# ScalarE issues part of the single-row transfers: eleven tiles fetched by rows, not eight

## The chip, the cores and the metric

The kernel runs on one core of a Trainium2 chip. The metric is the device time of one execution in microseconds (us): the median of the runs before the change is 726.54 us (three runs, 725.65 to 727.59). Engines are named as in the profile: PE is TensorE (PEld its weight loads), DVE VectorE, ACT ScalarE, POOL GpSimd, SP SyncE. A "q" behind a name is that engine's own queue: the instructions which it handles itself, among them the issue of transfers (DMAs).

## The reference

One layer of a graph network on 12,500 nodes with 128 features and 400,000 edges that are sorted by destination, followed by a residual and a layer norm.

```python
rbf = jnp.exp(-(distances[:, None] - centers) ** 2 / (2.0 * width * width))
cut = 0.5 * (jnp.cos(jnp.pi * distances / CUTOFF) + 1.0) * (distances <= CUTOFF)
W = (silu(rbf @ fw1 + fb1) @ fw2 + fb2) * cut[:, None]
messages = (h[src] @ pw + pb) * W
agg = segment_sum(messages, dst, num_segments=num_atoms)
h2 = h + (silu(agg @ mw1 + mb1) @ mw2 + mb2)
out = layernorm(x + h2)
```

Edges with a distance over 10 give nothing. The costly access is `h[src]`: one row of 512 bytes for each edge that counts.

## The kernel before

**Stages.** First `h @ pw + pb` is computed for all nodes and stored in HBM as the table `proj` (the first twelve tiles of edges still read the input's rows instead, which are multiplied in place). Meanwhile DVE drops the edges beyond the cutoff, chunk by chunk (seven chunks), and POOL stores the remaining ones packed; SP loads each packed chunk back (`pair`, L789), and from it come the source indices `srci` (L878), the local destinations `dl`, the cutoff factors and the distances, which are stored as `near_d` (L865).

**The loop.** What remains is 139 tiles of 512 edges, each of four rows of 128. The main loop (`for q in range(NL - 1)`) handles one tile a step:

- `fetch` (L1016): POOL fetches 128 rows of `proj` by an indirect DMA, four of them a tile, into a place of `quad_sb` (or of `x`). There are 21 places for the first 63 tiles and nine afterwards. `fetches` writes as many of them as have a free place by the planner's clock.
- `radials` (L1030): SP loads the distances of a pair of tiles (an "oct"), spread over partitions, into `d`, of which there are three buffers.
- `basis` (L1057, L1058): ACT squares and exponentiates them (`rbf`), for two octs at every fourth step. `first` (L1066): PE multiplies `rbf` with `fw1` into `ph`, of which there is one buffer. `silu` (L1072): ACT. `second` (L1080, L1083): PE, for the tile two steps ahead.
- `message` (L1094): DVE multiplies the filter in PSUM with the fetched rows. `place` (L1106): DVE writes a one-hot matrix of destinations. `sum_up` (L1126): PE sums messages by destination with it. `add` (L1160): DVE adds finished windows into `aggT`.
- Node stages run between (L1169 to L1224); SP loads and stores their tiles (L171).

**Tiles by rows.** For the eight tiles of `SINGLY` POOL makes three fetches, not four. The first 128 rows are brought row by row by SP: `one_by_one` (called once a step) writes single-row DMAs of 512 bytes into `dl_0` (L1006), one for each `A_ROW` = 0.58 us of the planner's clock. Their addresses are registers, loaded 32 at a time from `at_row` (L1002). DVE multiplies these rows in an instruction of its own (L1092).

**Order.** Each engine works its instructions in the order in which they stand in its queue. The order is set where the kernel is built, from the source's order by a scheduler. Hardware transfers of SP and ACT take eight completion semaphores ("places") in turn; a transfer that takes a place waits until the one before it in that place has landed. In the kernel before ACT issues six transfers, all near the start, and SP all others of that kind.

Of the kernel before, what the change touches and what calls it, by code (L numbers as in the profile page):

```python
# [10 lines left out]
F32 = mybir.dt.float32  # L11
BF16 = mybir.dt.bfloat16
I32 = mybir.dt.int32
U8 = mybir.dt.uint8
# [6 lines left out]
P = 128  # L21
# [8 lines left out]
QE = QT * P  # L30
# [51 lines left out]
def kernel(  # L82
# [37 lines left out]
    nc = tc.nc  # L120
    N, H = x.shape
# [44 lines left out]
    def node_dma(t0, sb, dr, store, n=None, eng=nc.sync):  # L166

        for a, m, k in alike(rows(t0, n)):
            d = dr[(t0 + a) * P:(t0 + a) * P + m * k].rearrange("(p t) f -> p t f", p=k)
            s = sb[:k, a:a + m]  # L170
            eng.dma_start(d, s) if store else eng.dma_start(s, d)  # L171

    raw = {}

    def load_rows(c):

        raw[c] = []
        of = (("r_src", src, I32), ("r_d", edge_weight, I32), ("r_dst", dst, I32))
        for name, ap, dt in of if c == 0 else of[1:] + of[:1]:
            t = work.tile([P, R_MAX], dt, name=name, bufs=2)[:, :ROWS[c]]  # L180
            v = ap[P * sum(ROWS[:c]):P * sum(ROWS[:c + 1])].rearrange("(r l) -> r l", r=P)
            nc.sync.dma_start(t, v if ap is not edge_weight else v.bitcast(I32))
            raw[c].append(t)
        if c == 0:
            raw[c].append(raw[c].pop(0))
# [12 lines left out]
    zero_i = keep.tile([P, 376], I32, name="zero_i")  # L198
    packed = dram.tile([LISTS, MW], I32, name="packed")

    def clear_packed(k, eng):
        a, b = CLEAR[k:k + 2]
        for i in range(LISTS if k == 0 else 3):
            v = packed[i, a:b].rearrange("(p w) -> p w", p=P)
            for w0 in range(0, (b - a) // P, 376):
                n = min(376, (b - a) // P - w0)
                eng.dma_start(v[:, w0:w0 + n], zero_i[:, :n])

    aggT = keep.tile([P, N], F32, name="aggT")

# [11 lines left out]

    def load(name, shape, ap, eng=nc.sync):
        t = keep.tile(shape, F32, name=name)
        eng.dma_start(t, ap)
        return t

    def load_bias(name, ap, eng=nc.sync):
# [5 lines left out]
    for t0 in range(0, 16, 4):  # L234
# [5 lines left out]
    loads = [(w1_sb[2 * a + h:2 * b - 1 + h:2, h, :], ap) for h in (0, 1)  # L240
             for a, b, ap in ((0, NUM_RBF, fw1), (NUM_RBF, KR, row(fb1)))]
# [152 lines left out]
    clock = [4.3]  # L394
# [106 lines left out]
    def pack_first():  # L501
# [124 lines left out]
        free.append(at)  # L626
        by_row = near_d[:p_d].rearrange("r (j p) -> (r j) p", j=2)
        for a, b in parts(D):
            nc.sync.dma_start(by_row[a:b], turned_d[a:b])
# [149 lines left out]
    def unpack(c):  # L779
# [6 lines left out]
        pair = work.tile([64, 3, 512], I32, name="pair", bufs=1)  # L786

        def listed(t, a, b, l0, l1):
            (nc.scalar if c < 1 else nc.sync).dma_start(t[a:b, :l1 - l0],  # L789
                              packed[l0:l1, (p0 + a) * 512:(p0 + b) * 512]  # L790
                              .rearrange("s (p w) -> p s w", w=512))

# [66 lines left out]
        def lengths():  # L859

            if c < 2:
                alike_in(1)
            one_of(length, 1)
            for a, b in parts(np_):
                nc.sync.dma_start(near_d[p0 + a:p0 + b], length[a:b].bitcast(F32))  # L865
            stored.add(c)

        def to_places(f, to):
# [119 lines left out]
        return own_sb[name, k]  # L988

    own_sb = {}  # L990
    singles, alone, rows_at, row_at = [], {}, [], [0.0]

    def one_by_one():

        row_at[0] = max(row_at[0], clock[0] - 8.0)
        while singles and row_at[0] < clock[0]:
            row_at[0] += A_ROW
            q, e, i = singles.pop(0)
            if e == 0:
                alone[q] = dl_0[:, SINGLY.index(q) % 4, :]  # L1000
            if e % AT_ONCE == 0:
                _, rows_at[:] = nc.values_load_multi_w_load_instructions(  # L1002
                    i[:, e:e + AT_ONCE], engines=[mybir.EngineType.SP], min_val=0,
                    max_val=(N - 1) * 4 * H, skip_runtime_bounds_check_because=
                    "sources are at most N - 1 where they are copied")
            nc.sync.dma_start(alone[q][e:e + 1, :].bitcast(U8),  # L1006
                              proj.rearrange("n f -> (n f)").bitcast(U8)[ds(rows_at[e % AT_ONCE], 4 * H)]
                              .rearrange("(o f) -> o f", o=1))

    def fetch(q, idx=None, table=None, js=range(QT)):  # L1010
        got = quad_sb[place_of(q) if q >= 0 else 0]
# [13 lines left out]
    def radial(o, lengths):  # L1025

        n = math.prod(lengths.shape) // QE
        d = work.tile([P, QE], F32, name="d", bufs=3)
        v = lengths.rearrange("(o h) e -> o h e", o=1)
        nc.sync.dma_start(d, v.to_broadcast([64, 2, QE]))  # L1030
        d_of[o] = d, n

    next_o = [0]
# [14 lines left out]
    def basis(o):  # L1048
        if o not in d_of:
            for q in quads(o):  # L1050
                while chunk_of(q) not in stored:
                    go_on(todo[0])
            radials(o + 1)
        d, n = d_of.pop(o)
        u = 2 * KR
        rbf = work.tile([P, QE], F32, name="rbf")
        nc.scalar.activation(rbf[:u], d[:u], AF.Square, bias=rbf_bias[:u], scale=rbf_scale[:u])  # L1057
        nc.scalar.activation(rbf[:u], rbf[:u], AF.Exp, scale=-1.0 / (2.0 * width * width))  # L1058
        rbf_of[o] = rbf, n
# [27 lines left out]
    def message(q, js=(0, QT)):  # L1087
        msg = own(q, "msg", 0)
        a, b = js
        if q in SINGLY and a == 0:  # L1090
            assert q in alone and all(s[0] != q for s in singles)
            nc.vector.tensor_mul(msg[:, 0, :], pu_of[q][:, :H], alone.pop(q))  # L1092
            a = 1
        nc.vector.tensor_mul(msg[:, a:b, :], pu_of[q].rearrange("p (j f) -> p j f", j=QT)[:, a:b, :],  # L1094
                             got_of[q][:, a:b, :])
        if b == QT:
            free.append(pu_of.pop(q))
            got_of.pop(q)
        return msg
# [285 lines left out]
    for k, t0 in enumerate(tiles):  # L1385
        if k + AHEAD_X < len(tiles):
            load_x(tiles[k + AHEAD_X], 4)
        if loads and k >= 4 and k % 2 == 0:
            nc.sync.dma_start(*loads.pop(0))
# [61 lines left out]
    for q in range(NL - 1):  # L1451
# [8 lines left out]
        if q >= CLEAR_Q:  # L1460
            clear()
        if loads_later and q >= 8:
            nc.sync.dma_start(*loads_later.pop(0))
# [92 lines left out]
    def everything():  # L1556
        nc.vector.memset(aggT, 0.0)
        def again(e0, seen):

            def column(ap, dt, name):  # L1560
                t = work.tile([P, QT], dt, name=name, bufs=1)
                nc.sync.dma_start(t, ap[ds(e0, QE)].rearrange("(j p) -> p j", p=P))
                return t

            idx = column(src, I32, "idx")
# [81 lines left out]
```

## Time and profile before

| | |
|---|---|
| runs | 726.54 us median, 725.65 to 727.59 |
| profiled execution | 726.45 us, its span 724.6 us |
| granted PE clock, mean | 0.912 |
| busy: PE, PEld | 586.3 us (81%), 463.4 us (64%) |
| busy: DVE, ACT, POOL | 560.9 us (77%), 403.9 us (56%), 532.7 us (74%) |
| fetches of POOL (L1016) | 405 + 95 + 48 = 548, 949 to 985 ns each |
| single rows of SP (L1006) | 1024, and 32 index loads |

"Busy" is the sum of an engine's instructions without register work, semaphores and the issue of transfers; those stand under the engine's "q". A group of the page's costliest instructions reads: line, engine, operation, what it writes from what, how many; then busy time and mean ns of one; then the engine's idle time just before them, with what ended most of it ("issue": nothing that the profile shows). A row of the timeline reads: start in us from the span's start, duration, engine, line, operation, tiles, how many in a row, and in brackets the idle time before it. A row of the windows reads: stretch, its length, then busy time and number of instructions for each engine named, and last granted clock, share of DMA and GB/s. A row of the waits reads: who waited for whom: us in total, times, longest. A row of one line's instructions reads: minimum, median and maximum in ns, then first and last start.

### The profile page before, as it was taken

What the parts mean: (1) busy time and instruction counts of PE and PEld (TensorE: products, weight loads), DVE (VectorE), ACT (ScalarE), POOL (GpSimd) and SP (SyncE); (2) the same over time, 40 slices, a digit from 0 to 9 for tenths busy, and PEclk for the clock granted to TensorE, in tenths of its full rate; (3) what the DMA queues carried; (4) which work ended last, traced back from release to release, by engine and by line L of the source; (5) the groups of instructions that cost most, each with busy time, mean ns of one, the idle gap of its engine ahead of it and who ended that gap; (6) DMA issues with size and microseconds to landing.
All of it is one profiled execution on the core that took longest, in us unless ns stands there. A gap on an engine that the chain in (4) does not pass through costs nothing.

```text
span 724.6 us, 13518 instructions
## 1 busy us (share of the span) xinstructions
PE 586.3 (81%) x3531; PEld 463.4 (64%) x3531; DVE 560.9 (77%) x1734; ACT 403.9 (56%) x573; POOL 532.7 (74%) x569
## 2 busy tenths in 40 slices
PE   6778868698889787598758896999896788797874
PEld 6666557676667566477536684877674566575753
DVE  8899799689999898699969794967556455564774
ACT  7547625364556566275444467557645744374683
POOL 6777777777777777777777777777777777777770
PEclk9998788899999899699988999899899988999996
DMA  8995442443334332433334344534443433345251
GB/s 278 324 314 182 146 125 75 112 115 96 100 90 127 98 94 74 147 93 89 98 102 113 100 125 121 158 98 138 115 112 98 141 98 109 102 122 149 57 154 56
DMA packets 53104, 91.38 MB, mean 126 GB/s; under 512 B 13824, under 2 KB 20576, under 8 KB 53018
## 3 DMA queue, kind: packets, MB, share of 16 engines
q1 hardware_dynamic: 34610, 53.34, 22.2%
q0 software_dynamic: 17840, 36.77, 20.5%
q8 instruction: 30, 0.49, 0.3%
q14 instruction: 56, 0.46, 0.2%
q10 hardware_dynamic: 568, 0.33, 0.2%
HBM read 74.59 MB, written 15.79 MB: 125 GB/s over the span
## 4 chain that ended last, share of the span: by engine, by line
DVE 29%; PE 19%; POOL 16%; DMA 14%; issue 14%; ACT 5%; DVEq 2%; SPq 1%; ACTq 0%; POOLq 0%
POOL quad L1016 14%; DMA quad<-proj,srci 8%; DVE hot L1106 6%; PE ph L1066 4%; PE bank L1083 4%; DVE msg L1094 3%; PE sums L1126 3%; PE bank L328 3%; POOL x L1016 2%; DVE aggT L1160 2%; DVE bank L492 2%; DVE nodes L496 2%; DVE r_d L486 2%; DMA x<-proj,srci 1%; DVEq L1135 1%
## 5 line engine op out<-in xcount | busy, mean ns | idle before, releaser
L1016 POOL DMA_INDIRECT quad<-proj,srci x405 | 384.5, 949 | 123.5 <-issue 98.8
L1083 PEld LDWEIGHTS bank<-fw_sb,s 128*128 128x128 f32 x1112 | 159.2, 206 | 61.5 <-issue 51.2
L1072 ACT ACTIVATE s<-ph 128x1024 f32<-128x1024 f32 x70 | 71.3, 1018 | 160.7 <-PE ph L1066 160.6
L1083 PE MATMUL bank<-fw_sb,s 128*128 128x128 f32 x1112 | 159.3, 290 | 0.0
L1066 PE MATMUL ph<-rbf,w_sb 102*128 102x512 f32 x278 | 138.8, 623 | 10.6 <-ACT s L1072 6.5
L1126 PEld LDWEIGHTS sums<-hot,msg 128*128 128x128 f32 x816 | 110.0, 201 | 50.1 <-issue 25.3
L1126 PE MATMUL sums<-hot,msg 128*128 128x80 f32 (+4 forms) x816 | 112.9, 284 | 10.5 <-DVE msg L1094 10.2
L1106 DVE TENSOR_SCALAR hot<-iota_n,dl,cut 128x80 f32<-128x80 f32 (+4 forms) x408 | 108.8, 339 | 14.7 <-PE sums L1126 12.9
L1016 POOL DMA_INDIRECT x<-proj,srci x95 | 90.8, 956 | 29.0 <-issue 24.1
L1080 PE MATMUL bank<-fb_b,ones_b 96*128 96x512 bf16 x139 | 56.1, 404 | 42.7 <-DVE msg L1094 15.6
L1094 DVE TENSOR_TENSOR msg<-bank,quad 128x512 f32<-128x512 f32 (+1 forms) x78 | 52.8, 677 | 43.0 <-DMA quad<-proj,srci 32.3
L1066 PEld LDWEIGHTS ph<-rbf,w_sb 102*128 102x128 f32 x278 | 49.2, 197 | 46.9 <-issue 35.2
L1160 DVE TENSOR_TENSOR aggT<-aggT,sums 128x80 f32 (+4 forms) x209 | 53.9, 258 | 28.0 <-PE sums L1126 11.9
L1057 ACT ACTIVATE rbf<-d,rbf_bias,rbf_scale 102x512 f32<-102x512 f32 x70 | 56.2, 803 | 33.3 <-DMA d<-near_d 33.3
L1016 POOL DMA_INDIRECT quad<-in_x_dram,srci x48 | 47.3, 985 | 15.4 <-issue 12.5
L328 PEld LDWEIGHTS bank<-pw_sb,xT 128*128 128x128 f32 (+1 forms) x292 | 41.6, 206 | 10.8 <-issue 5.5
L1094 DVE TENSOR_TENSOR quad<-bank,quad 128x512 f32<-128x512 f32 (+2 forms) x40 | 25.2, 633 | 28.2 <-DMA quad<-proj,srci 23.7
L1072 ACT ACT_TABLE_LOAD x36 | 46.2, 1283 | 0.6
L1126 PE MATMUL sums<-quad,quad 128*128 128x128 f32 (+3 forms) x296 | 44.9, 302 | 1.6 <-DVE quad L1094 1.5
L1058 ACT ACT_TABLE_LOAD x35 | 44.9, 1283 | 0.6
L1058 ACT ACTIVATE rbf<-rbf 102x512 f32<-102x512 f32 x70 | 44.1, 630 | 1.5
L1126 PEld LDWEIGHTS sums<-quad,quad 128*128 128x128 f32 x296 | 42.5, 220 | 2.4 <-DVE quad L1094 2.2
(268 smaller groups left out, 816.6 us busy)
## 6 DMA issues: line engine op xcount, KB each, us to landing
d<-near_d SPq DMA_DIRECT2D x70, 256.0 KB
dl<-proj SPq DMA_DIRECT2D x1024, 0.5 KB
x<-in_x_dram SPq DMA_DIRECT2D x46, 256.0 KB
quad<-proj,srci POOLq DMA_INDIRECT x405
proj<-hp SPq DMA_DIRECT2D x24, 256.0 KB
out_dram<-x SPq DMA_DIRECT2D x22, 256.0 KB
x<-proj,srci POOLq DMA_INDIRECT x95
r_d<-in_edge_weight_dram SPq DMA_DIRECT2D x5, 256.0 KB
```

The source lines that it names most:

```text
L328: nc.tensor.matmul(to[:m, k, :], lT[:, k * P:k * P + m], w, start=False, stop=(k == a + c - 1))
L1016: nc.gpsimd.indirect_dma_start(out=got[:, j, :], out_offset=None, in_=proj if table is None else table, in_offset=bass.IndirectOffsetOnAxi ...
L1057: nc.scalar.activation(rbf[:u], d[:u], AF.Square, bias=rbf_bias[:u], scale=rbf_scale[:u])
L1058: nc.scalar.activation(rbf[:u], rbf[:u], AF.Exp, scale=-1.0 / (2.0 * width * width))
L1066: nc.tensor.matmul(ph[:, h, :], w1_sb[:2 * KR, h, :], rbf[:2 * KR], start=True, stop=True)
L1072: nc.scalar.activation(s[:, :n], ph[:, :n], AF.Silu)
L1080: nc.tensor.matmul(pu, ones_b[:, :P], bias_b["fb2"].rearrange("k j f -> k (j f)"), start=True, stop=False)
L1083: nc.tensor.matmul(pu[:, j * H:(j + 1) * H], s[:, j * P:(j + 1) * P], fw2_sb, start=False, stop=(j == QT - 1))
L1094: nc.vector.tensor_mul(msg[:, a:b, :], pu_of[q].rearrange("p (j f) -> p j f", j=QT)[:, a:b, :], got_of[q][:, a:b, :])
L1106: nc.vector.tensor_scalar(hot[:, j, :wide(q)], iota_n[:, :wide(q)], dl[:, at[0], at[1]], cut[:, at[0], at[1]], op0=OP.is_equal, op1=OP.mult)
L1126: nc.tensor.matmul(pa[:, k * W:k * W + wide(q)], msg[:, j, :], hot[:, j, :wide(q)], start=(j % n == 0), stop=(j % n == n - 1))
L1160: nc.vector.tensor_add(to, to, pa[:, k * W:k * W + wide(q)])
```

## The change

`SINGLY` holds eleven tiles, spread over the loop. All hardware transfers go through `issue`, which counts them as they are written. When SP would write one whose number is 3 or 7 modulo 8 (`ACT_LANES`) and rows are pending, ACT writes a row first, which takes that number; so, counted in the order of writing, ACT's rows always have the numbers 3 and 7. Each engine loads its own indices: SP 32 at a time, ACT eight (`ACT_AT_ONCE`). `one_by_one` is called at three points of a step, with 2.8, 1.4 and 0 us subtracted from the planner's clock. The message of a tile by rows is unchanged.

```diff
-SINGLY = (22, 45, 62, 67, 86, 102, 118, 133)
+SINGLY = (20, 30, 43, 57, 68, 81, 95, 108, 118, 127, 135)
 A_ROW = .58
+ACT_LANES = (3, 7)
+ACT_AT_ONCE = 8
...
+    issued, singles, due = [0], [], {}
+
+    def issue(eng, to, frm):
+
+        while eng is nc.sync and (singles or due.get(nc.scalar)) and issued[0] % 8 in ACT_LANES:
+            one_row(nc.scalar, ACT_AT_ONCE)
+        issued[0] += 1
+        eng.dma_start(to, frm)
...
-                singles.extend((q, e, at_row[p:p + 1]) for e in range(P))
+                singles.append([q, 0, at_row[p:p + 1]])
...
-    def one_by_one():
+    def one_by_one(us):
 
         row_at[0] = max(row_at[0], clock[0] - 8.0)
-        while singles and row_at[0] < clock[0]:
+        while (singles or due.get(nc.sync)) and row_at[0] < clock[0] - us:
             row_at[0] += A_ROW
...
+            one_row(nc.sync, AT_ONCE)
+
+    def one_row(eng, n):
+
+        if not due.get(eng):
+            q, e, i = singles[0]
+            n = min(n, P - e)
             if e == 0:
-                alone[q] = dl_0[:, SINGLY.index(q) % 4, :]
+                alone[q], left[q] = dl_0[:, SINGLY.index(q) % 4, :], P
+            singles[0][1] += n
+            if e + n == P:
+                singles.pop(0)
+            _, at = nc.values_load_multi_w_load_instructions(
+                i[:, e:e + n], engines=[eng.engine], min_val=0, max_val=(N - 1) * 4 * H,
...
+            due[eng] = [(q, e + k, at[k]) for k in range(n)]
+        q, e, at = due[eng].pop(0)
+        left[q] -= 1
+        issue(eng, alone[q][e:e + 1, :].bitcast(U8),
+              proj.rearrange("n f -> (n f)").bitcast(U8)[ds(at, 4 * H)]
+              .rearrange("(o f) -> o f", o=1))
...
         radials(q // 2 + 5)
-        one_by_one()
+        one_by_one(2.8)
...
+        one_by_one(1.4)
         if q > NL - 5:
             keep_busy(2)
         sum_up(q, msg)
...
             add(k)
+        one_by_one(0.0)
         tail(q)
```

All other `nc.sync.dma_start(...)` of the kernel become `issue(nc.sync, ...)`.

More of the change, by code (lines that the diff above doesn't have):

```diff
@@ L170, in node_dma @@
             s = sb[:k, a:a + m]
-            eng.dma_start(d, s) if store else eng.dma_start(s, d)
+            issue(eng, d, s) if store else issue(eng, s, d)
     raw = {}
@@ L181, in load_rows @@
             v = ap[P * sum(ROWS[:c]):P * sum(ROWS[:c + 1])].rearrange("(r l) -> r l", r=P)
-            nc.sync.dma_start(t, v if ap is not edge_weight else v.bitcast(I32))
+            issue(nc.sync, t, v if ap is not edge_weight else v.bitcast(I32))
             raw[c].append(t)
@@ L224, in load @@
         t = keep.tile(shape, F32, name=name)
-        eng.dma_start(t, ap)
+        issue(eng, t, ap)
         return t
@@ L628, in pack_first @@
         for a, b in parts(D):
-            nc.sync.dma_start(by_row[a:b], turned_d[a:b])
+            issue(nc.sync, by_row[a:b], turned_d[a:b])
         yield 0.3
@@ L788, in listed @@
         def listed(t, a, b, l0, l1):
-            (nc.scalar if c < 1 else nc.sync).dma_start(t[a:b, :l1 - l0],
+            issue(nc.scalar if c < 1 else nc.sync, t[a:b, :l1 - l0],
                               packed[l0:l1, (p0 + a) * 512:(p0 + b) * 512]
@@ L864, in lengths @@
             for a, b in parts(np_):
-                nc.sync.dma_start(near_d[p0 + a:p0 + b], length[a:b].bitcast(F32))
+                issue(nc.sync, near_d[p0 + a:p0 + b], length[a:b].bitcast(F32))
             stored.add(c)
@@ L990 @@
     own_sb = {}
-    singles, alone, rows_at, row_at = [], {}, [], [0.0]
-    def one_by_one():
+    alone, left, row_at = {}, {}, [0.0]
+    def one_by_one(us):
         row_at[0] = max(row_at[0], clock[0] - 8.0)
-        while singles and row_at[0] < clock[0]:
+        while (singles or due.get(nc.sync)) and row_at[0] < clock[0] - us:
             row_at[0] += A_ROW
-            q, e, i = singles.pop(0)
-            if e == 0:
-                alone[q] = dl_0[:, SINGLY.index(q) % 4, :]
[L1001 to L1008, printed above, removed]
+            one_row(nc.sync, AT_ONCE)
[3 more added lines that the diff above has]
+            n = min(n, P - e)
+            if e == 0:
+                alone[q], left[q] = dl_0[:, SINGLY.index(q) % 4, :], P
[4 more added lines that the diff above has]
+                i[:, e:e + n], engines=[eng.engine], min_val=0, max_val=(N - 1) * 4 * H,
+                skip_runtime_bounds_check_because=
+                "sources are at most N - 1 where they are copied")
+            due[eng] = [(q, e + k, at[k]) for k in range(n)]
[4 more added lines that the diff above has]
+              .rearrange("(o f) -> o f", o=1))
     def fetch(q, idx=None, table=None, js=range(QT)):
@@ L1090, in message @@
         if q in SINGLY and a == 0:
-            assert q in alone and all(s[0] != q for s in singles)
+            assert q in alone and left[q] == 0
             nc.vector.tensor_mul(msg[:, 0, :], pu_of[q][:, :H], alone.pop(q))
@@ L1388 @@
         if loads and k >= 4 and k % 2 == 0:
-            nc.sync.dma_start(*loads.pop(0))
+            issue(nc.sync, *loads.pop(0))
         if k == 2:
```

8 lines of the change are left out of this document (4 added, 4 removed).

## The prediction

> **What bounds the kernel now.** First the page's head, its slices, and its costliest group.
>
> ```profile
> span 724.6 us, 13518 instructions
> ...
> POOL 6777777777777777777777777777777777777770
> ...
> L1016 POOL DMA_INDIRECT quad<-proj,srci x405 | 384.5, 949 | 123.5 <-issue 98.8
> ```
>
> POOL's digit is 7 from beginning to end, and its idle time before a fetch is "issue": it waits for nothing. The timeline of POOL and its fetches counted in two stretches give the pitch.
>
> ```profile
> 131.78 0.99 POOL L1016 DMA_INDIRECT quad<-proj,srci  x1 [0.30 <-issue]
> ...
> 704.33 0.94 POOL L1016 DMA_INDIRECT quad<-proj,srci  x1 [0.30 <-issue]
> ```
>
> ```profile
> 130.00:500.00 370.00, 276.37 (x291) 0.92 0.38 108
> 500.00:706.00 206.00, 155.27 (x164) 0.93 0.41 116
> ```
>
> 455 fetches stand in the two stretches; between the two shown lie 457 steps (453 fetches, four stores of packed rows): 572.55 / 457 = 1.253 us each. The last fetch ends at 705.27, and 19.3 us of span follow it. So POOL sets the end if the loop keeps up. Whether it does: the messages (L1094, one a tile) in the same stretches, all engines there, and the waits after 500 us.
>
> ```profile
> 130.00:500.00 370.00, 59.76 (x89) 0.92 0.38 108
> 500.00:706.00 206.00, 29.69 (x45) 0.93 0.41 116
> ```
>
> ```profile
> 500.00:706.00 206.00, 171.36 (x983) 129.88 (x983) 122.21 (x418) 118.92 (x173) 155.27 (x164) 0.93 0.41 116
> ```
>
> ```profile
> DVE msg L1094 <- DMA quad<-proj,srci: 32.3, 15, 4.7
> DVE quad L1094 <- DMA quad<-proj,srci: 23.2, 13, 3.2
> ```
>
> Before 500 us the loop goes at its own pace, 370 / 89 = 4.16 us a tile, while POOL needs 4 x 1.253 = 5.01: the loop eats POOL's lead and catches it near 500. After that DVE waits 55.5 us for landing fetches (28 times). That is the loop's **spare**: at most these 55.5; at least 206 - 45 x 4.16 = 19; PE's idle time there is 206 - 171.4 = 34.6. I take 35, PE being the busiest engine there. A loop that falls behind by less than its spare costs nothing at the end.
>
> SyncE issues all other transfers. Its instructions, two rows of its timeline, its waits over the span, and two landings from the chain that ended last:
>
> ```profile
> L1002 SPq TENSOR_LOAD <-at_row x32: 2107/2157/2347, 76.4 to 645.9; - x32
> ```
>
> ```profile
> L1006 SPq DMA_DIRECT2D dl<-proj x1024: 227/228/413, 79.1 to 664.1; - x171
> ```
>
> ```profile
> L1030 SPq DMA_DIRECT2D d<-near_d x70: 518/521/1362, 51.0 to 664.4; - x70
> ```
>
> ```profile
> 482.57 0.53 SPq L1030 DMA_DIRECT2D d<-near_d  x1
> 483.21 4.38 SPq L1006 DMA_DIRECT2D dl<-proj  x13
> ```
>
> ```profile
> SPq L171 <- ACT x L1224: 68.7, 16, 23.2
> SPq L789 <- DMA packed<-line,at_i: 30.3, 5, 9.2
> SPq L1006 <- DMA d<-near_d: 15.6, 31, 1.2
> ```
>
> ```profile
> 228.38 2.97 DMA d<-near_d
> ...
> 377.41 2.23 DMA dl<-proj
> ```
>
> A row takes 4.38 / 13 = 0.337 us of SP, an index load 2.16. From 79.1 to 664.4 SP has 585 us; 1024 rows are 345, 32 index loads 69, and some 142 other transfers (64 d loads at .56; 78 at .42, by the two pair loads in .77 shown below; each with a gap of .04) 68: 482 in all, so SP is busy 82% of the time. The 15.6 us in 31 waits of rows for a d load are the rule of places at work: a transfer may start only when the one before it in its place, eight transfers earlier, has landed. A row in its place finds 8 x .337 = 2.7 us past, more than 2.23; behind a d load it does not.
>
> **The change, part by part.** *Fetches.* Three more tiles by rows take three fetches off POOL: 3 x 1.253 = **-3.76 us**, certain if POOL stays the bound.
>
> *Rows.* 11 x 128 = 1408. In the built kernel SP still issues 1024, ScalarE 384, with 48 index loads of eight values. SP's own issue thus stays at 482. On ACT the nearest price of an index load is one of a single value:
>
> ```profile
> L1514 ACTq TENSOR_LOAD <-bad_i x1: 792/792/792, 699.6 to 699.6; - x1
> ```
>
> ```profile
> 699.62 0.38 ACT L1171 ACTIVATE zs<-bank 128x256 f32<-128x256 f32 x1 [1.09 <-PE bank L1169]
> ```
>
> ```profile
> ACT s L1072 <- PE ph L1066: 160.6, 58, 7.4
> ```
>
> .79, then; SP's 32 values cost 2.16; by the nearer I take 1.0 for eight. 48 x 1.0 + 384 x .26 (DMA and MOVE as on SP) = 148 us of ACT's queue. The two rows show how ACT's queue stands: zs waited 1.09 us for PE, and the load behind it came only as zs started, then ran beside it. So a row is **held by a waiting ACTIVATE** and is free beside a running one. ACT idles 160.6 us before the silus alone, so the issue by itself costs the loop little: 0 (all beside running work) to 20, taken as 5 in the pairs' sum below.
>
> The Trainium skill has it otherwise (Perfetto Trace Analysis, DVE / Act Engine Instruction): a vector or scalar instruction goes into a wait queue, and the sequencer takes the next one while the semaphores are still awaited. By that rule ACT's rows would not be held; the trace disagrees here, 699.62 against 699.6. What the rule would give in time is A's 722.8, below.
>
> *Places.* In the order in which the kernel is written ACT's rows take the fourth and eighth place of each turn. In the built program the eight places are dealt out in the scheduler's order instead, and there ACT's 384 rows lie in all eight, 39 to 61 in each. 301 of SP's transfers come in a place that ACT used last; 236 of these wait for an ACT row that the source wrote later than them, by 42 instructions in the median (a loop step has some 65). 299 ACT rows wait for one of SP's. So the two queues now run in **lockstep**, where before SP ran ahead.
>
> What it costs SP: I added up both queues in their built order with the prices above and nothing else (no compute on ACT), each transfer starting when its queue is free and its place has landed (2.23 after a row, 2.97 after others). Before: 481 us without places, 522 with them. That leaves 585 - 522 = 63 for waits on others' work; the table shows 30.3 of it at L789 and part of L171's 68.7. After: 485 without, **588** with places, 66 more than before. The bounds: if all 63 us of the old waits fall inside new ones, 588 - 585 = 3 us later; if none do, 66. With landings of 2.5 and 3.5 (the waits behind d loads allow this) it would be 85. Since ACT's compute, which holds rows, is not in the count, I go near the upper of the first two: **50**.
>
> A second way to it, by pairs of octs. The ACT timeline of a pair, one later second rbf, and all waits of that kind:
>
> ```profile
> 430.07 0.80 ACT L1057 ACTIVATE rbf<-d,rbf_bias,rbf_scale 102x512 f32<-102x512 f32 x1
> ...
> 432.72 0.80 ACT L1057 ACTIVATE rbf<-d,rbf_bias,rbf_scale 102x512 f32<-102x512 f32 x1
> ...
> 488.72 0.80 ACT L1057 ACTIVATE rbf<-d,rbf_bias,rbf_scale 102x512 f32<-102x512 f32 x1
> ```
>
> ```profile
> ACT rbf L1057 <- DMA d<-near_d: 33.3, 11, 7.1
> ```
>
> In 27 of 30 pairs of the new order the second d load stands, through its place or that of an SP transfer ahead of it, behind an ACT row just before the first rbf, 432.72 - 430.07 = 2.65 us ahead of the rbf that reads it. The row (.26), its landing (2.23), SP's work between (1.5 in the mean of the order) and the landing of d (2.97) make 6.96; less 2.65, and less up to 1.02 when the row goes out beside the silu ahead: 3.3 to 4.3 us late. Before, that load came early (482.57 for the rbf at 488.72: 6.15, less 2.97 = 3.2 to spare) and only 11 of 70 waited. PE notices when ACT's slack is gone, 160.6 / 58 = 2.8 a silu: .5 to 1.5 a pair, 16 to 46 over 31 pairs. With the late pair load of chunk 2 (below, 0 to 5 each for five chunks, 8 taken) and ACT's issue, 5, that is 29 to 59. Both ways lie about 45: 50 less the 3.2 us that SP was ahead is **47 us of lateness**, of which 35 go into the spare: **+12** at the end.
>
> *Pair loads.* They are hurried where a chunk begins:
>
> ```profile
> 117.96 0.77 SPq L789 DMA_DIRECT2D pair<-packed  x2
> ```
>
> ```profile
> 119.57 1.02 ACT L1072 ACTIVATE s<-ph 128x1024 f32<-128x1024 f32 x1 [0.94 <-PE ph L1066]
> ```
>
> ```profile
> 124.28 0.46 DVE L807 TENSOR_TENSOR two<-pair 44x256 int32<-44x256 int32 x1
> ...
> 129.25 0.24 DVE L878 CAST srci<-bank 128x88 int32<-128x88 f32 x1
> ```
>
> In the new order the load of 117.96 stands behind an ACT row that follows the silu of 119.57: 119.6 + three rows (.8) + 2.23 = 122.6, some 4.7 us later, and lands at 122.6 + .8 + 2.97 = 126.4, 2.1 after DVE began on it at 124.28. The indices, ready at 129.49, come 2.1 to 4.7 later, and POOL, which first reads them at 131.78, has 2.3 to spare: it may starve 0 to 2.4 us. I count 0 for POOL, the rest above.
>
> *Other edits.* Three calls of the pacing function instead of one spread SP's rows; their count is the same: nothing, and at most the 482 us shift within a step. The rows are written six steps or more (6 x 4.16 = 25 us) ahead of their message, so they themselves come in time if SP is late by less.
>
> Sum: the profiled run has span 724.6 and takes 726.45, the median of the runs is 726.54: 726.54 - 3.76 + 12 = **734.8**.
>
> **Rivals.**
> A, *the lateness stays inside the spare*: POOL bounds, 726.54 - 3.76 = **722.8**. For: 55.5 us of waits for fetches, ACT's 160.6 idle, the low end of either count (3, 29). It is also the time if ACT's rows are not held, as SP then finds them landed. Against: SP at 82% with its 63 us tied to others' work, and the order of places. Turning point: lateness 35.
> B, *even*: POOL starves 2.4 at chunk 2, and the lateness passes the spare by some 1: 722.8 + 3.4 = **726.2**. It needs two numbers to fall in a narrow band.
> C, *the holds feed one another*: an ACT row waits for an SP transfer that stands behind an SP row held by ACT. In the count ACT's own rows have 46 such changes of queue on the longest chain. With landings 2.5 and 3.5, excess 85, less 3, less the spare's low end 19: +63, **786**; slower still than forecast.
> D, *the rows do sit in two places*: then SP meets only its own transfers in six places, 6 x .337 = 2.02 us a turn against a landing of 2.23, .21 over 1024 / 6 = 171 turns: 36 us, which SP's 585 - 482 = 103 free us can take: **722.8** again. The built order speaks against it.
>
> **How the numbers follow.** The forecast, loop later than its spare, .57 (727.5 to 766: lateness 40 to 78); A with D .28; B .09; C .06. A measurement of this kernel tells .3% (2.2 us) from no change. Faster .28, same .09, slower .63. The likeliest case's own range is 728 to 764; the range for 8 in 10 takes in A's 722.8 with a little for the pitch: 721.5 to 764.
>
> **What would show it.** POOL: 545 fetches; in the forecast gaps before L1016 with DVE as releaser, or the last fetch later than 701.5. SP: waits of L1030, L171, L789 and L1006 for "DMA dl<-proj" of ten us and more in sum. ACT: rbf waits for d well over 33.3 us, most in the second rbf of a pair. The fetch waits of DVE after 500 us shrink from 55.5 toward zero. Wrong if SP shows no waits for dl, if ACT's rows come while an ACTIVATE waits, or if the messages keep 4.16 us before 500: then A. If POOL starves at 130 us alone, B.

## The result: 820 us, and the profile after

The changed kernel takes 820.28 us in the median of six runs (813.75 to 827.04), the kernel before 725.96 beside it: a ratio of 1.127, 95% interval 1.121 to 1.134. The forecast was 734.8. The profiled execution is the longest of the six, 827.04 with a span of 825.3; the ratio leaves it out, and it is some 7 us longer than the median. Its page begins:

```profile
span 825.3 us, 14353 instructions
...
PE 631.8 (77%) x3531; PEld 490.7 (59%) x3531; DVE 562.5 (68%) x1737; ACT 409.6 (50%) x574; POOL 529.6 (64%) x566
...
POOL 6777755777777767774075767477677777773300
```

DVE and ACT have the same work as before, POOL three fetches less; but POOL's row of sevens now has holes, and zeros at its end. POOL's timeline shows the largest hole and the last fetch (in brackets the idle time before an instruction and what ended it):

```profile
383.48 0.94 POOL L1038 DMA_INDIRECT quad<-proj,srci  x1 [0.30 <-issue]
393.55 0.99 POOL L482 DMA_INDIRECT packed<-line,at_i  x1 [9.13 <-DVE line L474]
412.06 1.47 POOL L1038 DMA_INDIRECT quad<-proj,srci  x1 [17.52 <-DVE msg L1116]
...
770.45 0.94 POOL L1038 DMA_INDIRECT quad<-proj,srci  x1 [0.30 <-DMA quad<-proj,srci]
```

The last fetch ends at 771.39, where before it was 705.27: **66.1 us** later. POOL's twelve stops after the first 60 us, counted over the usual 0.30 us between fetches, are 69.9 us together; less 3.8 for the three fetches that are gone, that is the difference. Behind it 53.9 us of span follow, not 19.3: another **34.6**. The two make the 100.7 us between the spans. So POOL no longer sets the end; the loop does, and where its lateness reaches POOL, POOL stops. The first part of the last message starts at 806.78 (705.59 before): the loop is 101.2 us late there, and the last fetch has ended 35.4 us earlier (0.3 before). The messages (L1116, one a tile; L1094 before) in the two stretches, with 51.36 and 32.44 us of DVE's time:

```profile
130.00:500.00 370.00, 51.36 (x77) 0.82 0.32 88
500.00:772.00 272.00, 32.44 (x48) 0.85 0.38 107
```

One a 4.81 us before 500 (4.16 in the kernel before) and one a 5.67 after it (206 / 45 = 4.58 in the kernel before). DVE's waits for landing fetches, 55.5 us after 500 before the change, do not appear in the list of that stretch any more, nor in that of the whole run: fetches lie ready. What the loop waits for stands in the waits:

```profile
ACT s L1094 <- PE ph L1088: 117.5, 43, 6.0
...
ACT rbf L1079 <- DMA d<-near_d: 106.6, 30, 6.8
...
ACT rbf L1079 <- DMA dl<-proj: 25.5, 15, 3.5
...
ACT xT L963 <- DMA dl<-proj: 17.5, 5, 8.8
```

and of SyncE alone (all its transfers now have line 149):

```profile
SPq L149 <- DMA dl<-proj: 155.4, 109, 6.3
SPq L149 <- ACT x L1246: 34.7, 9, 16.7
```

SyncE waits 155 us, 109 times, for rows in the places of its transfers, a wait that its table before did not have among its largest. ACT's rbf waits 106.6 + 25.5 us, not 33.3. How they hang together shows in 23 us of the timelines of ACT and SP, and the same stretch of the chain that ended last:

```profile
726.11 1.02 ACT L1094 ACTIVATE s<-ph 128x1024 f32<-128x1024 f32 x1 [3.87 <-PE ph L1088]
726.18 0.57 ACTq L149 DMA_DIRECT2D dl<-proj  x2
...
733.62 0.50 ACTq L149 DMA_DIRECT2D dl<-proj  x1
734.17 0.81 ACT L1079 ACTIVATE rbf<-d,rbf_bias,rbf_scale 102x512 f32<-102x512 f32 x1 [1.98 <-DMA dl<-proj]
...
740.43 0.82 ACT L1079 ACTIVATE rbf<-d,rbf_bias,rbf_scale 102x512 f32<-102x512 f32 x1 [3.51 <-DMA d<-near_d]
```

```profile
717.97 9.66 SPq L149 DMA_DIRECT2D dl<-proj  x9
727.69 0.37 SPq L149 DMA_DIRECT2D x<-in_x_dram  x1
728.16 0.53 SPq L149 DMA_DIRECT2D d<-near_d  x1
728.79 7.58 SPq L149 DMA_DIRECT2D dl<-proj  x18
736.42 0.36 SPq L149 DMA_DIRECT2D x<-in_x_dram  x1
736.88 0.52 SPq L149 DMA_DIRECT2D d<-near_d  x1
```

```profile
722.29 3.79 PE ph L1088 x4
726.18 1.21 DMA dl<-proj
728.16 3.77 DMA d<-near_d
731.95 1.65 DMA dl<-proj
735.00 1.28 ACT L1080
736.88 3.53 DMA d<-near_d
```

Read from the top: silu waits 3.87 us for PE and starts at 726.11; the rows behind it go out at 726.18, not earlier. By the chain one of them lands 1.21 us later, at 727.39, and only then does SP issue the last of nine rows, on which it has spent 9.66 us (3.0 at .337 each), its transfer of 727.69, and d at 728.16. That lands at 731.93; the row behind it goes at 731.95 and lands at 733.60; an ACT row goes at 733.62, and rbf, which stands behind this row and reads nothing of it, has waited 1.98 us. The next d goes out at 736.88 and lands at 740.41; rbf starts at 740.43. SyncE is at work in 486 of the 693 us from its first row to its last (gaps under .15 us counted as work), so its queue is not full.

### The profile page after: what moved, and what is told of

Read it like the earlier page. It is cut to its first block, busy times and chain, and to the rows that moved or that the text cites. A ratio compares the mean times of both kernels' runs of the same rounds, so it can differ in the third digit from the quotient of the medians.

```text
span 825.3 us, 14353 instructions
## 1 busy us (share of the span) xinstructions
PE 631.8 (77%) x3531; PEld 490.7 (59%) x3531; DVE 562.5 (68%) x1737; ACT 409.6 (50%) x574; POOL 529.6 (64%) x566
## 4 chain that ended last, share of the span: by engine, by line
PE 25%; DMA 24%; issue 13%; ACT 10%; DVE 8%; SPq 7%; POOL 6%; ACTq 5%; DVEq 0%; POOLq 0%
PE ph L1088 11%; DMA d<-near_d 10%; POOL quad L1038 6%; SPq L149 6%; DMA dl<-proj 5%; PE sums L1148 4%; PE bank L1105 4%; ACTq L149 4%; ACT s L1094 2%; ACT rbf L1079 2%; DMA x<-in_x_dram 2%; DMA quad<-proj,srci 2%; PE bank L1191 2%; DMA pair<-packed 2%; PE bank L339 1%
## 5 line engine op out<-in xcount | busy, mean ns | idle before, releaser
L1038 POOL DMA_INDIRECT quad<-proj,srci x403 | 383.3, 951 | 172.3 <-issue 101.2
L1088 PE MATMUL ph<-rbf,w_sb 102*128 102x512 f32 x278 | 171.8, 750 | 82.9 <-ACT s L1094 69.5
L1105 PEld LDWEIGHTS bank<-fw_sb,s 128*128 128x128 f32 x1112 | 163.9, 212 | 43.8 <-issue 36.8
L1105 PE MATMUL bank<-fw_sb,s 128*128 128x128 f32 x1112 | 163.4, 295 | 0.0
L1148 PEld LDWEIGHTS sums<-hot,msg 128*128 128x128 f32 x816 | 124.2, 222 | 54.1 <-issue 37.7
L1088 PEld LDWEIGHTS ph<-rbf,w_sb 102*128 102x128 f32 x278 | 57.7, 230 | 132.9 <-ACT s L1094 73.4
L1094 ACT ACTIVATE s<-ph 128x1024 f32<-128x1024 f32 x70 | 71.2, 1017 | 121.9 <-PE ph L1088 117.5
L1148 PE MATMUL sums<-hot,msg 128*128 128x80 f32 (+4 forms) x816 | 122.8, 301 | 8.9 <-DVE msg L1116 8.7
L1079 ACT ACTIVATE rbf<-d,rbf_bias,rbf_scale 102x512 f32<-102x512 f32 x70 | 56.7, 810 | 135.0 <-DMA d<-near_d 106.6
L1102 PE MATMUL bank<-fb_b,ones_b 96*128 96x512 bf16 x139 | 58.0, 418 | 25.8 <-DVE msg L1116 8.7
L1116 DVE TENSOR_TENSOR msg<-bank,quad 128x512 f32<-128x512 f32 (+1 forms) x78 | 52.5, 673 | 11.7 <-ACT rbf L1079 5.4
L339 PEld LDWEIGHTS bank<-pw_sb,xT 128*128 128x128 f32 (+1 forms) x292 | 41.4, 206 | 12.8 <-issue 6.1
L339 PE MATMUL bank<-pw_sb,xT 128*128 128x128 f32 (+1 forms) x292 | 42.5, 292 | 0.8 <-ACT xT L963 0.6
L1148 PE MATMUL sums<-quad,quad 128*128 128x128 f32 (+3 forms) x296 | 41.2, 285 | 0.5 <-DVE quad L1116 0.4
L1246 ACT ACTIVATE x<-x,by,rs 128x128 f32<-128x128 f32 x94 | 38.5, 482 | 5.9 <-DVE by L1232 2.1
```

Of the source, the lines that this page charges most:

```text
L339: nc.tensor.matmul(to[:m, k, :], lT[:, k * P:k * P + m], w, start=False, stop=(k == a + c - 1))
L1038: nc.gpsimd.indirect_dma_start(out=got[:, j, :], out_offset=None, in_=proj if table is None else table, in_offset=bass.IndirectOffsetOnAxi ...
L1088: nc.tensor.matmul(ph[:, h, :], w1_sb[:2 * KR, h, :], rbf[:2 * KR], start=True, stop=True)
L1094: nc.scalar.activation(s[:, :n], ph[:, :n], AF.Silu)
L1102: nc.tensor.matmul(pu, ones_b[:, :P], bias_b["fb2"].rearrange("k j f -> k (j f)"), start=True, stop=False)
L1105: nc.tensor.matmul(pu[:, j * H:(j + 1) * H], s[:, j * P:(j + 1) * P], fw2_sb, start=False, stop=(j == QT - 1))
```

## The experiments

The differences are to the kernel before, run beside each. For all in this table the kernel before took 724 to 728 us on the same chip.

| run | tiles | rows of SP / ACT | us | to before |
|---|---|---|---|---|
| the change | 11 | 1024 / 384 | 820.3 | +94 |
| all_on_sp | 11 | 1408 / 0 | 824.6 | +99 |
| eight_tiles | 8 | 768 / 256 | 752.9 | +27 |
| more_lead | 11 | 1024 / 384 | 794.4 | +69 |
| act_loads | 8 | 1024 / 0 | 725.8 | 0 |
| bursts_b | 11 | 944 / 464 | 784.4 | +59 |
| bursts_no_lead_b | 11 | 944 / 464 | 791.4 | +66 |
| pair_lead_b | 11 | 1024 / 384 | 823.0 | +97 |
| before_pair_lead_b | 8 | 1024 / 0 | 726.0 | 0 |

The other runs fell on chips on which the kernel before took 1077 to 1106 us (one execution 1961), with stops in all queues that nothing in the profiles taken there explains. There each is compared only with before on the same chip, and its size is not set beside the first table: bursts +59 us, bursts_no_lead +46, pair_lead +89, before_pair_lead -6, four_lanes +77 and in its repeat +81, eight_one_lane +29, one_lane +110, nine_on_sp +17 twice.

**All rows on SyncE.**

```diff
-ACT_LANES = (3, 7)
+ACT_LANES = ()
-A_ROW = .58
+A_ROW = .40
```

> The eleven tiles stay, but ScalarE issues no row: SyncE issues all 1408 (their planned spacing goes from 0.58 to 0.40 us, so that they are written in time). Theory 1, the places: what costs the 94 us is that SyncE's transfers wait for rows in ScalarE's queue and ScalarE waits for what SyncE then brings late; without rows on ScalarE these waits are gone, SyncE's waits for dl<-proj fall from 155 us to under 30, and the time is 725 to 765, the upper end because SyncE then has 482 + 384 x 0.337 = 611 us of issue for some 590. Theory 2, the number of rows: 1408 single rows are too many for the transfer engines whoever issues them; the time stays above 800. Theory 3, the issue itself: ScalarE's queue is too full with 384 rows and 48 loads; the time falls as in theory 1, and the run act_loads tells the two apart.

824.6 us. That is theory 2's time, but not for its reason. The waits for rows are gone: of all that waits for dl only 5.6 us of DVE and 0.6 of POOL are listed. What takes their place is SyncE's own issue. Its rows, index loads, and a stretch of its timeline:

```profile
L149 SPq DMA_DIRECT2D dl<-proj x1408: 227/228/585, 79.7 to 757.6; - x176
```

```profile
478.71 1.23 SPq L149 DMA_DIRECT2D dl<-proj  x4
480.04 0.52 SPq L149 DMA_DIRECT2D d<-near_d  x1
480.66 9.05 SPq L149 DMA_DIRECT2D dl<-proj  x26
489.90 0.37 SPq L149 DMA_DIRECT2D x<-in_x_dram  x1
490.36 0.53 SPq L149 DMA_DIRECT2D d<-near_d  x1
```

SP is at work in 637 of the 678 us from its first row to its last (gaps under .15 us counted as work), and rbf waits 170.6 us for d. In the changed kernel it was at work in 486 of 693. So with eleven tiles SyncE alone brings d late, and nearly the same time with ScalarE's help is another limit: 384 rows less to issue, and 167 us more of waiting.

**Eight tiles.**

```diff
-SINGLY = (20, 30, 43, 57, 68, 81, 95, 108, 118, 127, 135)
+SINGLY = (22, 45, 62, 67, 86, 102, 118, 133)
```

> The change with the eight tiles of before: ScalarE issues rows by the same rule, and SyncE has fewer than the 1024 of before, some 740. Theory 1: the places still tie the two queues together, so the time is 770 to 820, though SyncE has a quarter less to issue. If instead SyncE's load together with the waits is what binds (482 us of issue and the holds), the time falls to 727 to 745.

752.9 us, between the two expectations: 27 us slower than before with the same rows in all, and 256 fewer of them on SyncE. Sharing the rows costs by itself. SyncE's largest wait, and a row of POOL's timeline:

```profile
SPq L149 <- DMA dl<-proj: 94.1, 70, 8.9
```

```profile
399.95 0.97 POOL L1038 DMA_INDIRECT quad<-proj,srci  x1 [15.33 <-DVE msg L1116]
```

The row of POOL is its fetch for tile 72. From tile 63 on nine places are used, so this fetch needs the place of tile 63, and waits for its message. Where it was taken before the change (373.21, below) it did not wait. POOL has two more stops, of 5.99 us before a packed line at 121.82 and of 5.11 before the first fetch with new indices at 143.08. The three are 25.5 us over the usual 0.30 each; POOL's last fetch ends 27.7 us later than before, again 0.3 us ahead of its message, and that is all that the run has lost.

**One more buffer and an earlier d.**

```diff
-        d = work.tile([P, QE], F32, name="d", bufs=3)
+        d = work.tile([P, QE], F32, name="d", bufs=4)
...
-        radials(q // 2 + 5)
+        radials(q // 2 + 6)
```

> The changed kernel with one more buffer for d (four, not three), each d load written two steps (some 8 us) earlier; rows as in the change. Theory 1 in its simple form (a d load comes late by the hand-over row, landing, d load, some 4 to 7 us, and nothing else is late): the waits of rbf for d fall from 107 us to under 40 and the time to 740 to 770. If the two queues bind each other throughout (each of SyncE's transfers only as early as ScalarE's rows allow, whatever is written first), the time stays within 2% of 820.

794.4 us, outside both expectations. The waits of rbf for d fall to 57.8 us, not under 40, and the late pair load grows (41.4 us of DVE, 23.5 in the change). SyncE still waits 141.9 us for rows. An earlier d helps by 26 us; the queues stay tied.

**Loads in ScalarE's queue in place of rows.**

```diff
+            for n in ((8, 1) if loads_[0] % 8 == 0 else (1,) if loads_[0] % 8 in (3, 6) else ()):
+                nc.values_load_multi_w_load_instructions(
+                    singles[0][2][:, :n], engines=[nc.scalar.engine], ...)
```

> Eight tiles, all rows on SyncE as before; where the change would put a row on ScalarE, ScalarE gets register loads of about the same time in its queue and no transfer: one of eight values and one of a single value in place of eight rows, and single ones at the third and sixth, some 0.8 us each. Theory 1: 726 to 740, since no place is shared. Theory 3 (the issue on ScalarE costs the time): 770 or more.

725.8 us, but the run doesn't test what it was meant to. The trace holds none of these loads: nothing reads their registers, and they were dropped when the kernel was built, so that only 183 waits are left in ScalarE's queue. What the run does show is that the rest of the edit costs nothing: it has the changed code, the count and the three calls of the pacing function, with eight tiles and every row on SyncE. Against it eight_tiles differs in who issues 256 of the rows, with their index loads, and takes 27 us more.

The cost of the issue itself stays untested by a run, and it may not be small. The page of the changed kernel has, for the chain that ended last:

```profile
PE 25%; DMA 24%; issue 13%; ACT 10%; DVE 8%; SPq 7%; POOL 6%; ACTq 5%; DVEq 0%; POOLq 0%
```

ScalarE's own queue, its row transfers and index loads, is 5% of that chain, some 37 us in its pieces, and 0% of the chain of the kernel before. How much of this would stay if the two queues had separate places is not shown.

**Bursts.** ScalarE's rows behind each silu, up to eight at once, and both d loads of the next pair behind this pair's second exp; bursts_no_lead has the first part alone, pair_lead the second alone, before_pair_lead the second part in the kernel before.

```diff
-        while eng is nc.sync and (singles or due.get(nc.scalar)) and issued[0] % 8 in ACT_LANES:
-            one_row(nc.scalar, ACT_AT_ONCE)
...
             silu(octs(q))
+            some_rows(8)
...
                     basis(o)
+            radials(q // 4 * 2 + 8)
```

> Eleven tiles; ScalarE issues up to eight rows at a time, right behind each silu (two bursts in a pair of octs), instead of one wherever SyncE's count is 3 or 7; and both d loads of the next pair are written at one point, behind the second exp of this pair. In the built order some 285 of SyncE's transfers still come in a place that ScalarE used last (301 in the change), but the row that a d load stands behind, directly or through SyncE's queue, now lies 6 to 27 us of ScalarE's work ahead of the rbf that reads it, where it was 2.5. Theory 1 (what costs is a d load that waits for a row which ScalarE reaches only just before that d is needed): rbf's waits for d fall from 107 us to under 40, and the time is 722 to 740. If a shared place costs whatever stands in it: 800 or more. If SyncE's 1024 rows with holds of any kind are too much for it: 760 to 800.

> The bursts alone, with the d loads written where they were before. The row that a second d load stands behind is again close to the rbf in part of the pairs. Theory 1: between the two, 735 to 780, with waits of rbf for d of 50 to 90 us.

> The rows of the change (one in two of eight of SyncE's transfers), and only the d loads moved: both of the next pair written behind the second exp, a pair ahead of use. In the built order the place of most of them still follows a ScalarE row that stands close ahead of the rbf. Theory 1: little is won, 790 to 825. If it is the writing point of d that counts and not the row that it stands behind: under 750.

> The kernel before with only that move of the d loads, all rows on SyncE. Without ScalarE's rows nothing is behind them: 722 to 730, rbf's waits for d (33 us before) under 33 or about the same. It shows how much of the run bursts is due to the move alone.

These four came first on a chip where before took 1094 us, and were run again:

> The kernel of the run bursts again, since the kernel before took 1094 us where that one was measured, with stops of TensorE of up to 30 us that nothing in the profile explains. Eleven tiles; up to eight of ScalarE's rows right behind each silu; both d loads of the next pair written behind the second exp of this one. Theory 1 (what costs is a d load behind a row that ScalarE reaches only just before d is needed): rbf's waits for d under 40 us, 722 to 740. If a shared place costs whatever stands in it: 800 or more. If SyncE's rows with holds of any kind are too much for it: 760 to 800.

> The kernel of bursts_no_lead again, for the same reason: bursts, with the d loads where the change has them. Theory 1: 735 to 780, waits of rbf for d of 50 to 90 us.

> The kernel of pair_lead again, for the same reason: rows as in the change, both d loads of the next pair written behind the second exp. Theory 1: 790 to 825, as the rows still stand between. If the writing point of d counts by itself: under 750.

> The kernel of before_pair_lead again, for the same reason: the kernel before, only with that move of the d loads. 722 to 730; rbf's waits for d of 33 us or less.

784.4, 791.4, 823.0 and 726.0. The mechanism that theory 1 named is gone in bursts_b: rbf waits 3.4 us for d. Of the change's 94 us, 59 remain. 784.4 lies in the range of the third theory (SyncE's rows with holds of any kind, 760 to 800), which this run doesn't tell from a tie on ScalarE's side. In bursts_no_lead_b time and waits both missed: 791.4 for 735 to 780, and 47.4 us of rbf's waits for d for 50 to 90. The waits of ACT in bursts_b:

```profile
ACT aggT L226 <- DMA dl<-proj: 35.2, 10, 5.6
ACT zs L1197 <- DMA dl<-proj: 34.8, 8, 7.6
ACT s L1098 <- DMA dl<-proj: 31.9, 9, 5.4
ACT rbf L1083 <- DMA dl<-proj: 25.3, 7, 5.3
ACT x L1250 <- DMA dl<-proj: 18.9, 6, 6.0
```

and one burst in its timeline:

```profile
560.11 1.00 ACT L1098 ACTIVATE s<-ph 128x1024 f32<-128x1024 f32 x1
560.70 6.34 ACTq L147 DMA_DIRECT2D dl<-proj  x8
567.09 1.65 ACT L1250 ACTIVATE x<-x,by,rs 128x128 f32<-128x128 f32 x4 [5.98 <-DMA dl<-proj]
```

Eight rows that cost .26 us each to issue (.235 and a MOVE of .029 in their rows) take 6.34, since their places are held by rows not yet landed; the ACTIVATEs behind them, which read none of these, wait 146.1 us in the five groups shown. It is the same tie from its other side: SyncE still waits 123.5 us for rows, and now ScalarE waits for the places too. Theory 1 as it was put, that only a d behind a late row costs, falls. pair_lead_b agrees with it (823.0, in 790 to 825), and before_pair_lead_b shows that the move of d by itself is worth nothing: no rbf waits for d there, 33.3 us did before, and the time is the same. So these waits of rbf cost the kernel before nothing.

**How many rows on which queue.** The four runs on the slower chips, with eleven tiles on four places, eight on one, eleven on one, and nine tiles on SyncE alone in the kernel before (the runs on one place have `ACT_LANES = (3,)`; one_lane also `A_ROW = .48`):

```diff
-ACT_LANES = (3, 7)
+ACT_LANES = (1, 3, 5, 7)
```

```diff
-SINGLY = (22, 45, 62, 67, 86, 102, 118, 133)
+SINGLY = (22, 45, 57, 67, 81, 95, 108, 121, 135)
-A_ROW = .58
+A_ROW = .50
```

> Eleven tiles; ScalarE issues a row wherever SyncE's count is 1, 3, 5 or 7, so that each queue has 704 rows. SyncE's own issue falls from 482 to some 375 us. In the built order 321 of its transfers come behind a ScalarE row, 28 of them written before it (236 in the change). If SyncE's load is the half of the cost that eleven tiles add to eight: 755 to 790. If it is the number of ScalarE's rows that costs, as eight tiles with 256 of them cost 27 us: 27 x 704 / 256 = 74 us over 722, some 797, or more.

> Eight tiles; ScalarE takes one place of eight: 144 rows, SyncE 880. 133 of SyncE's transfers come behind a ScalarE row (half of eight_tiles'). SyncE's spare shrinks from 173 idle us toward the 98 of before. If the cost goes with ScalarE's rows: 726 + 27 x 144 / 256 = 741. If SyncE's load at the same number of holds decides: 745 to 770. If the loop's spare (35 us) takes half of the lateness in: 726 to 735.

> Eleven tiles; ScalarE takes one place of eight: 192 rows, SyncE 1216 (planned spacing 0.48 us). All on SyncE (1408 rows) took 825 with SyncE idle for 41 of 678 us, 1024 with 384 on ScalarE took 820 with 208 idle. If both costs add over SyncE's queue (1216 x 0.337 + 39 x 2.16 + 68 = 562 us of issue, and half of the holds, some 60): 800 to 825, no better than either. If the two trade off with a best point between: 760 to 795.

> The kernel before with nine tiles by rows, all 1152 on SyncE (planned spacing 0.50 us), none on ScalarE. One fetch less is 1.25 us of POOL. SyncE's issue rises by 128 x 0.337 + 4 x 2.16 = 52 us to 534, with 41 of holds by its own places 575 of some 590. If SyncE still keeps up: 724.5 to 726. If it is full, as all_on_sp says of 1408: 730 to 745.

> The kernel of four_lanes again, since the kernel before took 1082 us where that one was measured: 704 rows on each queue, 28 of SyncE's transfers behind a ScalarE row that was written later. If SyncE's load is half of what eleven tiles add: 755 to 790. If ScalarE's number of rows costs: 797 or more. The run on the slower chip was 77 us over before, so some 803.

> The kernel of nine_on_sp again, for the same reason: nine tiles, 1152 rows, all on SyncE. If SyncE keeps up: 724.5 to 726. If it is full: 730 to 745; the run on the slower chip was 17 us over before, so some 743.

Ratios to before on the same chip: four_lanes 1.072 (1.066 to 1.079) and 1.075 (1.066 to 1.085), eight_one_lane 1.028 (1.023 to 1.033), one_lane 1.103 (1.099 to 1.109), nine_on_sp 1.018 (1.014 to 1.023) and 1.017 (1.010 to 1.025). All six intervals lie above 1, those of nine_on_sp with a middle under 2%, so none of these counts pays there. The two ends show in ACT's waits, of four_lanes_b and then of one_lane:

```profile
ACT rbf L1079 <- DMA dl<-proj: 103.6, 14, 19.8
```

```profile
ACT rbf L1079 <- DMA d<-near_d: 315.7, 43, 23.0
```

With half of the rows on ScalarE its ACTIVATEs wait for places; with 1216 rows on SyncE it is d that comes late. But a row costs SyncE more on such a chip: its MOVEs take 133 ns in the mean in before_pair_lead and 29 in before_pair_lead_b, the same kernel. That a lighter SyncE does not help (four_lanes) and that a ninth tile on SyncE alone already costs (nine_on_sp) is therefore shown for those chips alone; on an undisturbed chip neither was measured.

## Why the prediction was wrong

**What held.** The sign; POOL's fetches (545, 3.8 us less); that the rows do not lie in two places; that SyncE's waits for dl are the sign of it (155.4 us); that the late d load is mostly a pair's second (rbf's idle time is 94.5 us before the second of a pair, 40.5 before the first); that a row waits behind a waiting ACTIVATE: 726.18 against 726.11, after 3.87 us of waiting; of ScalarE's 63 waits for PE of over 1 us, a row goes out within .3 us of the start that ends them in 41. This speaks again against the wait queue of the Trainium skill (Perfetto Trace Analysis, DVE / Act Engine Instruction).

**The step that failed first: SyncE's excess, "50".** It was set between 3 and 66, from a count of both queues with no compute on ACT. SyncE starts its rows from 80.4 to 773.4 us, 693 us for the same 1024 rows where it had 585: an excess of **108**. Some 9 us of it are two tiles of the loop (the last tile by rows is 135, not 133); the rest is the lateness of the loop itself, 103 us at tile 135, where **47** had been forecast. The count's upper end rested on rows that ScalarE issues as soon as it can; but a row also waits until its ACTIVATE starts, that one waits for PE, PE for the silu or the rbf ahead of it, and the rbf for a d that SyncE issues once the row has landed. That circle is rival C (holds that feed one another), which was given .06 and 786 us, from landing times. What was already on the page spoke for it: the forecast itself said that ACT's compute was missing from the count, and still stayed under the count's upper end.

**The second way, "0.5 to 1.5 a pair", failed with it.** It was to be what PE notices of a late d. PE's idle time before the matmuls into ph stands on the page, after and before:

```profile
L1088 PE MATMUL ph<-rbf,w_sb 102*128 102x512 f32 x278 | 171.8, 750 | 82.9 <-ACT s L1094 69.5
```

```profile
L1066 PE MATMUL ph<-rbf,w_sb 102*128 102x512 f32 x278 | 138.8, 623 | 10.6 <-ACT s L1072 6.5
```

It is 72.3 us more, 2.1 for each of 35 pairs. The working took d as the only late load; rbf's waits for d and dl together are 132.1 us, where 33.3 stood before. ACTIVATEs behind rows that wait for places (25.5 us of rbf, 17.5 of xT) were not in it at all. And the same matmuls are busy 33.0 us longer, a term that the working had at nothing. The two, 72.3 and 33.0, are together about the lateness of 101 us; that they make it up is an addition, not a test.

**The spare, "35", was used up, and it has a limit that the forecast left out.** In the changed kernel DVE waits for no fetch, so the 55.5 us of waits from which the spare was taken are gone, and the last message is still 101.2 us late. The loop is 86 us late at tile 95 already, which the kernel before reaches at 501 us, so a spare counted after 500 us could not have held it. POOL's stops make no fetch late: every tile's last fetch ends at least 21.6 us before its message. The larger ones follow the loop, as POOL has nine places from tile 63 on. Before the change the fetch of tile 72 and the message of tile 63 stood so:

```profile
373.21 0.97 POOL L1016 DMA_INDIRECT quad<-proj,srci  x1 [0.31 <-issue]
```

```profile
357.73 0.68 DVE L1094 TENSOR_TENSOR msg<-bank,quad 128x512 f32<-128x512 f32 x1
```

373.21 - 358.41 = 14.8 us is all that the loop can fall behind POOL there before POOL stops. The changed loop is 54.5 us late at tile 60; POOL, itself late by then through its earlier stops, stands 17.52 us for that message (412.06 above), after 9.13 for a packed line that DVE brings late. What this limit costs shows in eight_tiles, where POOL sets the end again: 42 us of lateness at tile 60, a stop of 15.33, and with the two at the first chunks nearly all of the 27.7 us. The buffer count was in the code and in the text ahead of the prediction; it should have been a limit on the spare.

**The smaller terms.** POOL's loss at the first chunks was put at 0 to 2.4 us; the two stops before 145 us are 7.4 and 5.6. ScalarE's load of eight values was put at 1.0 us and takes 0.81 in the mean; its issue as a whole was put at 5 us of lateness, and 37 us of the chain that ended last are its queue's. The granted clock was not forecast: .847 over the span, not .912, and the 278 matmuls into ph take 750 ns in the mean, not 623; in busy time, where overlapping records count once, this is the 33.0 us above.

**What stays open.** How the 67 us between eight tiles and eleven divide between SyncE's 1024 rows and ScalarE's 384; four_lanes points to ScalarE's, on the slower chips alone. How the 27 us of eight tiles divide between shared places and the issue on ScalarE. And whether the rows would pay in places of their own: no version with places kept apart was run, so that the tie is shown by the waits (present in every kernel in which both queues issue rows, absent with 1408 rows on one) and not by its removal. No version beat the kernel before.

## What to carry to other kernels

Two queues that share a ring of completion semaphores hold each other up wherever their order in the ring differs from the order in which they get to it; count the ring in the order of the built program, not of the source. A second queue's issue time is not the whole price: what stands behind each transfer, on both queues, has to be priced with the compute that holds it, since a chain of holds that passes through both queues repeats each period. And a loop's spare ends where its producer runs out of buffers.

## What was not expected of the hardware

The matmuls into ph, all of one shape, took 591 to 1222 ns in both kernels. The granted clock that the trace records goes between 1.0 and 0.5 in both. Where it is 1.0 all through one of these matmuls, it takes 594 ns in the mean before (259 of them) and 599 after (185); where it is 0.5 all through, 1080 before (15) and 1090 after (75). The four of 722.29 above, 3.79 us together behind 4.41 us without a matmul, all run at 0.5. From kernel to kernel their mean rises with PE's idle time just before them on the page: 623 ns at 10.6 us (before), 632 at 24.5 (bursts_b), 671 at 47.7 (eight_tiles), 750 at 82.9 (the change). So in these kernels a loop that stopped more before these matmuls also had slower ones; no run was made to show what lowers the clock.

On three of the chips used, the kernel before took about half as long again as on the others; the profile of before_pair_lead there has waits of up to 30 us on ScalarE that it puts down to "remote", which it does not show. Kernels that were clearly slower elsewhere were slower there too, and those run on both kinds of chip kept their size within 20 us (bursts +59 and +59, bursts_no_lead +46 and +66, pair_lead +89 and +97, before_pair_lead -6 and 0).
